# A pre-norm graph network layer on one core: the last result of a batch is joined and stored behind the next batch's first convolution, and GpSimd's transfers are planned as issued at once

## The chip, the cores and the metric

The kernel runs on one core of one Trainium2 chip. All arithmetic is in fp32. The metric is the time of one execution on the device in microseconds; lower is better. The times given are medians over several executions, and a profile is that of one further execution, taken by the hardware profiler.

In the rows of the profile, PE is TensorE (PEld is its loading of weights), DVE is VectorE, ACT is ScalarE, POOL is GpSimd and SP is SyncE. A row of a timeline gives start, length, engine, line, operation, output and inputs with their shapes, how many instructions the row stands for, and in brackets the idle time before it with what ended it.

## The reference, cut to what matters

There are 64 graphs of 256 nodes with 256 features, and a 256 x 256 adjacency matrix for each.

```python
h = jnp.maximum(_layernorm(x, axis=-1), 0.0)
x = x + gnn(h, adj, ...)

def gnn(x, mask, ...):                       # x is h here
    xc = jnp.transpose(x, (0, 2, 1))
    h = jax.nn.relu(_bn(_conv1d(xc, conv1_w, 0), ...))       # 1 tap
    h = _bn(_conv1d(h, conv2_w, 8), ...)                     # 17 taps
    x_conv = jnp.transpose(jax.nn.relu(h + xc), (0, 2, 1))
    s = x @ w_se.T + b_se                                    # 3 numbers per node
    sq = jnp.sum(s * s, axis=-1)
    dist = sq[:, :, None] + sq[:, None, :] - 2.0 * jnp.einsum('bnd,bmd->bnm', s, s)
    A = jnp.exp(-dist) * mask
    msg = jax.nn.relu(x @ w_msg.T + b_msg)
    x_nmp = jnp.einsum('bnm,bmd->bnd', A, msg)
    x_in = jnp.concatenate([x_conv, x_nmp], axis=-1)
    gi = x_in @ w_ih.T + b_ih                                # 768 = r, z, n
    gh = x @ w_hh.T + b_hh
    r = jax.nn.sigmoid(gi_r + gh_r)
    z = jax.nn.sigmoid(gi_z + gh_z)
    nn_ = jnp.tanh(gi_n + r * gh_n)
    return (1.0 - z) * nn_ + z * x
```

## The kernel before, in words

**Tiling.** A pair is two graphs (`G = 2`, 32 pairs), a batch is eight graphs or four pairs (`PB = 4`, `NB = 8` batches, numbered 0 to 7). In this text, pairs 0 to 3 are the pairs of a batch.

**The convolution of a batch.** The 17-tap convolution is done for a whole batch by a transform of length 16. VectorE splits and transforms the input (`split`, `forward`), TensorE multiplies 16 bins, each in up to three kinds of product (`begin` and `complete`, lines 908 to 937), and VectorE transforms back (`branch_back`, `odd_back`, `q_back`, `p_back`, then `join`). The transformed inputs are named `U`, `V`, `Sv` and `PT` in the trace, the transformed results `Yu` and `Yv`, and `T` is scratch. The filters of the 16 bins are worked out once, in a prologue, and lie in DRAM as `filt`. In each batch SP loads them, 256 KB at a time, into nine slots `wb` (`load_kinds`, line 872); 47 such loads make one batch. A slot is loaded again when the product that reads it is done. In the second half of the batch the same nine slots are scratch of the gates (`roles`, line 1037). At the batch's end `give` (line 1043) releases them, and `load_kinds` fills all nine for the next batch. So the first products of a batch, `acc<-Sv,wb`, can't start until the gates of the batch before have let the slots go and SP has loaded them.

**The graph work of a pair** runs beside it: `message` (features and the three numbers `s`), `embed` (transposes of them, `zT`), `affinity` (the exponential `e`, times `adj`), `aggregate` (`xnm`). From the second batch on, `hT`, the transposed normalised input of a pair, is made with DMAs: ScalarE writes `hh` (`turn_h`), a DMA transposes it into `halves`, four DMAs sort it back into `hh` (`sort_h`), and two ScalarE copies join 16-bit halves to `hT` (`join_h`). The adjacency matrix of a pair goes a similar way: a DMA transpose to `halves`, a store to DRAM (`halves_d`), four loads to `adjh`, two ScalarE copies to `adj` (`turn_adj`, `load_adj`, `join_adj`).

**The gates of a pair** (`gates`, line 1144) are twice `seven` (line 1118), which computes a 2 x 2 block product with seven instead of eight products. It holds one PSUM tile `acc`, copies it negated into a second one (ScalarE's `acc<-acc`), evicts an `aux` tile into the slot `e`, and goes on adding. ScalarE then does the nonlinear parts, and writes the result of the pair in 16-bit halves into `back`.

**The last step of a pair** (`finish`, line 1174). SP issues a DMA transpose `gn<-back`. Two ScalarE copies `back<-gn` of 1024 16-bit values for each partition join the halves. GpSimd issues, for each of the two graphs, a DMA that adds `x` from DRAM into `back` (`back<-in_x_dram`, 256 KB) and one that stores it (`out<-back`, 256 KB). The last of the 32 pairs is finished with TensorE transposes instead.

`back` and `gn` are single tiles, so the next pair's gates wait for these copies and stores.

**What sets the order.** The program isn't issued as written. A recorder (line 250) takes every operation as a task with its reads and writes, plans all of them with a list scheduler, and emits them in that order; it is why all instructions carry the one line L370 in the profile. It plans twice: the prologue, and all batches together. Each task has a modelled cost and a due time `late`, which is worked out backwards from the modelled start of each TensorE instruction. Among tasks that could start first on an engine it takes the one due first. A DMA is placed on one modelled channel (`self.dma`), and on one of two sets of eight lanes, one for GpSimd and one for all others. A DMA that isn't due within `CALM = 20` us of the point that TensorE has reached is held back until the modelled channel is free, less 1 us (lines 419 and 420):

```python
                if self.pace + self.CALM < t.late < math.inf:
                    now = max(now, self.dma - 1.0)
```

The planned order is fixed for each engine. On the chip, an engine runs its instructions in that order, and waits on semaphores for what it reads or overwrites.

**The order around the change.** In the loop over batches (lines 1248 to 1382), `finish` of the batch's first three pairs stands behind their gates (lines 1328, 1346, 1365). That of pair 3 stands at the start of the next batch, ahead of all products (line 1252). Products end with `complete(7)` (line 1298), behind which `p_back` and `q_factors` follow.

Of the kernel before, what the change touches and what calls it, by code (L numbers as in the profile page):

```python
# [14 lines left out]
U16 = mybir.dt.uint16  # L15
AF = mybir.ActivationFunctionType
ALU = mybir.AluOpType
# [10 lines left out]
class Slots:  # L28
# [3 lines left out]
    def __init__(self, t, A, n, E):  # L32
        self.t = t.rearrange("p (a c n e) -> p a c n e", a=A, c=2, n=n)
# [216 lines left out]
class Recorder:  # L250
# [15 lines left out]
    def __init__(self, nc):  # L266
        self.nc, self.tasks, self.live, self.masks = nc, [], {}, {}
        self.first, self.planned, self.dma = None, 0, 2.3
        self.lanes = [deque([0.0] * self.LANES) for _ in range(2)]
        self.free = dict.fromkeys(self.LAG, 0.0)  # L270
        for name in ("tensor", "vector", "scalar", "gpsimd", "sync"):
            setattr(self, name, Proxy(self, name))

# [59 lines left out]
    def record(self, engine, op, args, kw):  # L333
        method = getattr(getattr(self.nc, engine), op)
        out = kw["out"] if "out" in kw else args[0]
        ins = [v for v in list(args) + list(kw.values()) if isinstance(v, bass.AP) and v is not out]
        n = 1
        for s in out.shape[1:]:
            n *= s
        size = 0  # L340
        if op.startswith("dma"):
            if "transpose" in op:
                size, cost = 2.5, self.TURN
            elif "accum_op" in kw:
                size, cost = 2.3, 1.0
            else:
                k = max(self.share(out, ins[0]), 10 if engine == "gpsimd" else 1)
                run = min(self.run(v) for v in (out, ins[0]))
                size = n * out.shape[0] * WIDTH[out.dtype] * 16 / k / 330e3 * max(1, 1400 / run)
                cost = 0.35 if k > 10 and run > 1024 else 0.62  # L350
        elif engine == "tensor":
            cost = n / 597 + 0.006
            if op == "transpose":
                cost = out.shape[-1] / 1170
            elif args[1].shape[0] < 32:
                cost = 0.23
        elif engine == "vector":
            cost = {"bn_stats": 0.33, "bn_aggr": 0.07}.get(op, n / 960 + 0.07)
            if op == "tensor_mul" and n == 256:
                cost = 0.5  # L360
        elif engine == "scalar":
            cost = n / 1400 + (0.2 if op == "activation" else 0.12)
            if out.dtype == U16:
                cost = n / 860
            elif len(out.shape) == 3 and op == "activation" and n == 256:
                cost = 0.49
        else:
            cost = 1.1 if self.planned == 0 else 7.0 if ALU.pow in args else 2.0
        k = len(self.tasks)
        self.tasks.append(Task(engine, lambda: method(*args, **kw), cost, size, self.first))  # L370
        if self.first is not None:
            self.first += 1
        for v in ins:
            self.access(k, v, False)
        self.access(k, out, True)
        return k
# [7 lines left out]
    def plan(self, fixed=False):  # L384

        T, new = self.tasks, range(self.planned, len(self.tasks))
        self.planned = len(T)
        total = 0.0
        for k in new:
            t = T[k]  # L390
            for p in t.preds:
                T[p].succs.append(k)
            if t.engine == "tensor":
                t.late = total
                total += t.cost
        for k in reversed(new):
            t = T[k]
            for s in t.succs:
                t.late = min(t.late, T[s].late - self.lag(t, T[s]) - self.cost(t))
            if t.first is not None:  # L400
                t.late = t.first - 1e6
        ready, free = {e: [] for e in self.LAG}, self.free
        left = {}

        def enable(k):
            at = max((T[p].done + self.lag(T[p], T[k]) for p in T[k].preds), default=0.0)
            ready[T[k].engine].append((at, k))
        for k in new:
            left[k] = sum(p in left for p in T[k].preds)
            if not left[k]:  # L410
                enable(k)
        order = []
        self.pace = 0.0

        def when(e, at, t):
            now = max(free[e], at)
            if t.size:
                now = max(now, self.lanes[e == "gpsimd"][0])
                if self.pace + self.CALM < t.late < math.inf:
                    now = max(now, self.dma - 1.0)  # L420
            return now

        def commit(k, e, at, now):
            t = T[k]
            ready[e].remove((at, k))
            t.begin = now
            free[e] = t.done = now + t.cost
            if e == "tensor":
                self.pace = max(self.pace, t.late)
            if t.size:  # L430
                if t.cost == self.TURN:
                    free[e] = max(free[e], self.dma + 1.1)
                self.dma = max(self.dma, now + 1.6) + t.size
                t.done = self.dma + 1.1
                lanes = self.lanes[e == "gpsimd"]
                lanes.popleft()
                lanes.append(t.done)
            order.append(k)
            for s in t.succs:
                left[s] -= 1  # L440
                if not left[s]:
                    enable(s)
        while fixed and len(order) < len(new):
            k = new[len(order)]
            e = T[k].engine
            at = next(at for at, j in ready[e] if j == k)
            commit(k, e, at, max(free[e], at, self.lanes[e == "gpsimd"][0] if T[k].size else 0.0))
        while len(order) < len(new):
            best = []
            for e in ready:  # L450
                cand = [(when(e, at, T[k]), T[k].late, k, at) for at, k in ready[e]]
                if cand:
                    now = min(cand)[0]
                    best.append((now, min(c[1:] for c in cand if c[0] <= now + 1e-9), e))
            now, (_, k, at), e = min(best)
            commit(k, e, at, now)
        return order
# [25 lines left out]
def kernel(  # L483
# [18 lines left out]
    nc = Recorder(tc.nc)  # L502
    P = 128
    B, N, D = x.shape
    G = 2
    GB = 8
    PB = GB // G
    NB = B // GB
    NP = B // G
    DC = D // P  # L510
# [71 lines left out]
    def rows(t, g):  # L582
        return t[g].rearrange("(b h c) d -> h b (c d)", h=L // 2, c=MC)

    def row_tile(t, g):
        return t[:, g * MC:(g + 1) * MC, :].rearrange("p c d -> p (c d)")
# [5 lines left out]
    def chunk(t, g, c):  # L592
        return t[:, g * N + c * P:g * N + (c + 1) * P]
# [121 lines left out]
    p = aux()  # L715
# [457 lines left out]

    def finish(i):
        if i + 1 < NP:
            y = back.rearrange("p (q d) -> p q d", d=D)
            t = gn_tile.rearrange("p c n -> p (c n)").bitcast(U16)
            nc.sync.dma_start_transpose(out=t.rearrange("p (k n) -> p k n", n=P), in_=back.bitcast(U16))
            v = y.bitcast(U16).rearrange("p q (c d j) -> p j c q d", c=DC, j=2)
            u = t.rearrange("p (c j q d) -> p j c q d", j=2, c=DC, d=P)  # L1180
            for j in range(2):
                nc.scalar.copy(v[:, j], u[:, j])
            for g in range(G):
                nc.gpsimd.dma_start(out=row_tile(y, g), in_=rows(x, G * i + g), accum_op=ALU.add)
                nc.gpsimd.dma_start(out=rows(out, G * i + g), in_=row_tile(y, g))
            return
        for g in range(G):
            p = aux()
            for c in range(MC):
                for dc in range(DC):  # L1190
                    transpose(p[:, c * D + dc * P:c * D + (dc + 1) * P], chunk(tr_tile[:, dc], g, c))
            nc.vector.tensor_add(row_tile(x_rows, g), p, row_tile(x_rows, g))
            nc.sync.dma_start(out=rows(out, G * i + g), in_=row_tile(x_rows, g))

    FIRST = PARTS[1][1]
    steps = deque((m, g) for g in range(FIRST) for m in range(len(PASSES)))
# [48 lines left out]
    gn_tile, tr_tile = (late.tile([P, DC, W], FP, name=n) for n in ("gn", "tr"))  # L1245
    back = late.tile([P, DC * W], FP, name="back")
    hh, halves = (late.tile([P, 2 * MC, W], U16, name=n) for n in ("hh", "halves"))
    for b in range(NB):
        i = b * PB
        nxt = i + PB  # L1250
        if b > 0:
            finish(i - 1)
# [43 lines left out]
        if b > 0:  # L1296
            load_adj(i + 2)
        complete(7)
        fft.p_back(Yu, T)
        fft.q_factors(Yu)  # L1300
        roles()
# [128 lines left out]
```

## Time and profile before

| what | before |
| --- | --- |
| median of 3 executions | 1739.63 us (1739.28 to 1740.79) |
| profiled execution | 1734.89 us |
| its span, first to last instruction | 1733.1 us |
| mean granted TensorE clock | 0.986 |
| TensorE matmuls busy | 1678.7 us (97%) |
| VectorE busy | 1461.7 us (84%) |
| ScalarE busy | 1038.5 us (60%) |
| GpSimd busy | 254.6 us (15%) |
| DMA moved | 260.90 MB, mean 151 GB/s |
| `back<-gn` copies on ScalarE | 62, 1348 ns each |
| `back<-in_x_dram` on GpSimd's queue | 62, 256 KB each, median 7.5 us from issue to landing |
| `out<-back` on GpSimd's queue | 62, 256 KB each, median 4.5 us |
| `wb<-filt` on SP's queue | 376, 256 KB each |

Busy times are those of the profiled execution. The engines run beside each other, so their shares of the span don't add up to 100%. TensorE is the one that is nearly always busy; its remaining idle time, 54 us in all, is spread over the eight batches. The time of the profiled execution is the one to compare with its span; the median is of other executions of the same program.

### The profile page before, as it was taken

The page shows a single profiled execution, that of the slowest core. Times are in us where ns is not written, and L with a number is a line of the kernel's source. Part 1 is how long each engine was busy: PE and PEld are TensorE (multiplying, and loading weights), DVE is VectorE, ACT ScalarE, POOL GpSimd, SP SyncE. Part 2 cuts the span into 40 slices and gives each one's busy share as a digit, 9 for nine tenths or more (in the row PEclk, how much of TensorE's full clock was granted, in tenths as well). Part 3 has the DMA queues.
Part 4 walks back from the last instruction along what each step waited for, and adds up shares of the span by engine and source line. Part 5 has one row for each costly group of instructions (what it writes and reads, how often), then busy time and mean ns, then how long its engine had stood idle before and what let it go on. Part 6 is the DMA issues. An engine that isn't in the chain of part 4 may idle for free.

```text
span 1733.1 us, 26180 instructions
## 1 busy us (share of the span) xinstructions
PE 1678.7 (97%) x8998; PEld 1427.0 (82%) x8998; DVE 1461.7 (84%) x3400; ACT 1038.5 (60%) x1949; POOL 254.6 (15%) x246
## 2 busy tenths in 40 slices
PE   8999999999999999999999999999999999999996
PEld 6788878888789788888888887897888978898885
DVE  7959999699897898798986988968988889879443
ACT  3536666487656766576654766567566665547543
POOL 3211320002110221102110031102211022100010
PEclk9999999999999999999999999999999999999998
DMA  9982475865668465684558655684656847374122
GB/s 222 284 277 75 102 141 118 278 147 117 131 161 258 103 138 122 205 202 92 127 110 255 166 99 119 146 269 101 141 114 188 231 90 136 69 250 113 22 52 49
DMA packets 326457, 260.90 MB, mean 151 GB/s; under 512 B 204808, under 2 KB 252196, under 8 KB 326323
## 3 DMA queue, kind: packets, MB, share of 16 engines
q1 hardware_dynamic: 293818, 213.72, 46.6%
q0 software_dynamic: 29568, 42.84, 13.0%
q10 hardware_dynamic: 2937, 2.66, 0.7%
q8 instruction: 71, 1.16, 0.3%
q14 instruction: 63, 0.52, 0.1%
HBM read 156.03 MB, written 43.78 MB: 115 GB/s over the span
## 4 chain that ended last, share of the span: by engine, by line
PE 87%; DMA 5%; DVE 5%; ACT 2%; issue 1%; SPq 0%; POOL 0%; ACTq 0%; DVEq 0%; POOLq 0%
PE acc L370 60%; PE aux L370 27%; DMA wb<-filt 2%; DVE V L370 1%; DMA filt<-fo 1%; DVE T L370 1%; DMA hh<-halves 1%; DMA T<-in_x_dram 0%; ACT e L370 0%; DVE acc L370 0%; DVE tr L370 0%; DVE e L370 0%; DVE gn L370 0%; DMA x<-in_x_dram 0%; ACT back L370 0%
## 5 line engine op out<-in xcount | busy, mean ns | idle before, releaser
L370 PE MATMUL acc<-wb,w_ih 128*128 128x256 f32 x768 | 192.4, 379 | 0.0
L370 POOL DMA_DIRECT2D back<-in_x_dram x62 | 62.8, 1147 | 772.0 <-ACT back L370 772.0
L370 PEld LDWEIGHTS acc<-wb,w_ih 128*128 128x128 f32 x768 | 145.9, 190 | 19.8
L370 POOL TENSOR_TENSOR rstd<-rstd,neg_half 128x4 f32<-128x4 f32 x32 | 96.0, 2999 | 390.6 <-DVE shift L370 225.4
L370 PE MATMUL aux<-wb,w_x 128*128 128x256 f32 x576 | 141.3, 384 | 4.0 <-ACT e L370 3.2
L370 PE MATMUL acc<-wb,w_x 128*128 128x256 f32 x576 | 137.0, 382 | 7.5 <-DVE acc L370 7.5
L370 DVE SCALAR_TENSOR_TENSOR V<-T,V 128x128 f32<-128x128 f32 (+2 forms) x448 | 140.5, 375 | 0.0
L370 PEld LDWEIGHTS acc<-wb,w_x 128*128 128x128 f32 x576 | 107.9, 190 | 34.5 <-DVE acc L370 14.2
L370 PEld LDWEIGHTS aux<-wb,w_x 128*128 128x128 f32 x576 | 108.1, 191 | 23.6 <-ACT e L370 6.0
L370 PE MATMUL acc<-V,wb 128*128 128x128 f32 x1024 | 119.9, 277 | 5.0 <-DMA wb<-filt 3.8
L370 PE MATMUL aux<-w_msg,hT 128*128 128x259 f32 x512 | 121.5, 382 | 1.2 <-ACT fo L370 1.2
L370 DVE TENSOR_TENSOR T<-Yv 128x512 f32<-128x512 f32 (+1 forms) x80 | 42.5, 580 | 94.9 <-ACT Yv L370 94.3
L370 PEld LDWEIGHTS acc<-V,wb 128*128 128x128 f32 x1024 | 117.6, 194 | 5.9 <-DMA wb<-filt 4.4
L370 PEld LDWEIGHTS acc<-U,wb 128*128 128x128 f32 x1024 | 116.9, 192 | 0.9
L370 PE MATMUL acc<-U,wb 128*128 128x128 f32 x1024 | 117.1, 275 | 0.0
L370 PE MATMUL aux<-hT,w_c 128*128 128x512 f32 x224 | 106.9, 596 | 3.9 <-ACT e L370 2.7
L370 PE MATMUL acc<-wb,w_hh 128*128 128x256 f32 x384 | 110.0, 381 | 0.1
L370 PE MATMUL acc<-Yv,w_ih 128*128 128x256 f32 x384 | 109.6, 381 | 0.1
L370 PEld LDWEIGHTS aux<-w_msg,hT 128*128 128x128 f32 x512 | 96.3, 190 | 16.1 <-ACT fo L370 1.6
L370 PE MATMUL acc<-hT,w_hh 128*128 128x256 f32 x384 | 106.5, 384 | 3.2 <-ACT acc L370 3.2
L370 PE MATMUL acc<-xnm,w_ih 128*128 128x256 f32 x384 | 104.8, 382 | 0.0
L370 ACT COPY back<-gn 128x1024 uint16<-128x1024 uint16 x62 | 81.0, 1348 | 37.8 <-DMA gn<-back 37.8
(179 smaller groups left out, 3849.9 us busy)
## 6 DMA issues: line engine op xcount, KB each, us to landing
wb<-filt SPq DMA_DIRECT2D x376, 256.0 KB
back<-in_x_dram POOLq DMA_DIRECT2D x62, 256.0 KB, 7.5
out_dram<-back POOLq DMA_DIRECT2D x62, 256.0 KB, 4.5
x<-in_x_dram SPq DMA_DIRECT2D x58, 256.0 KB
halves_d<-halves SPq DMA_DIRECT2D x28, 512.0 KB
adjh<-halves_d SPq DMA_DIRECT2D x112, 128.0 KB
hh<-halves SPq DMA_DIRECT2D x108, 128.0 KB
filt<-fo POOLq DMA_DIRECT2D x18, 252.0 KB, 6.6
```

Source lines behind the costliest of these rows:

```text
L370: self.tasks.append(Task(engine, lambda: method(*args, **kw), cost, size, self.first))
```

## The change

Two things change. First, the rule that holds a DMA back until the modelled channel is free no longer applies to DMAs that GpSimd issues. Second, `finish` of a batch's pair 3 issues only its DMA transpose where it stood. Its two copies, two adds and two stores are a function `deliver`, which for pair 3 is recorded behind `complete(7)` of the next batch. While it is recorded, each of its tasks gets one more predecessor in the plan, `behind`, the ScalarE task recorded last before it (the last copy of `complete(7)`). That predecessor counts for the planner's order alone and makes no semaphore. For the other pairs, `finish` calls `deliver` at once, with the same operations in the same order as before.

```diff
@@ Recorder.__init__
         self.free = dict.fromkeys(self.LAG, 0.0)
+        self.last, self.behind = {}, None
@@ Recorder.record
         self.tasks.append(Task(engine, lambda: method(*args, **kw), cost, size, self.first))
+        self.last[engine] = k
+        if self.behind is not None:
+            self.tasks[k].preds.add(self.behind)
@@ Recorder.plan
             if t.size:
                 now = max(now, self.lanes[e == "gpsimd"][0])
-                if self.pace + self.CALM < t.late < math.inf:
+                if e != "gpsimd" and self.pace + self.CALM < t.late < math.inf:
                     now = max(now, self.dma - 1.0)
@@ finish
         if i + 1 < NP:
-            y = back.rearrange("p (q d) -> p q d", d=D)
             t = gn_tile.rearrange("p c n -> p (c n)").bitcast(U16)
             nc.sync.dma_start_transpose(out=t.rearrange("p (k n) -> p k n", n=P), in_=back.bitcast(U16))
-            v = y.bitcast(U16).rearrange("p q (c d j) -> p j c q d", c=DC, j=2)
-            u = t.rearrange("p (c j q d) -> p j c q d", j=2, c=DC, d=P)
-            for j in range(2):
-                nc.scalar.copy(v[:, j], u[:, j])
-            for g in range(G):
-                nc.gpsimd.dma_start(out=row_tile(y, g), in_=rows(x, G * i + g), accum_op=ALU.add)
-                nc.gpsimd.dma_start(out=rows(out, G * i + g), in_=row_tile(y, g))
+            if i % PB < PB - 1:
+                deliver(i)
             return
+
+    def deliver(i):
+        y = back.rearrange("p (q d) -> p q d", d=D)
+        t = gn_tile.rearrange("p c n -> p (c n)").bitcast(U16)
+        v = y.bitcast(U16).rearrange("p q (c d j) -> p j c q d", c=DC, j=2)
+        u = t.rearrange("p (c j q d) -> p j c q d", j=2, c=DC, d=P)
+        for j in range(2):
+            nc.scalar.copy(v[:, j], u[:, j])
+        for g in range(G):
+            nc.gpsimd.dma_start(out=row_tile(y, g), in_=rows(x, G * i + g), accum_op=ALU.add)
+            nc.gpsimd.dma_start(out=rows(out, G * i + g), in_=row_tile(y, g))
@@ the loop over batches
         complete(7)
+        if b > 0:
+            nc.behind = nc.last["scalar"]
+            deliver(i - 1)
+            nc.behind = None
         fft.p_back(Yu, T)
```

## The prediction

> **What bounds the kernel now.** I read the page's first part, then TensorE's timeline for its idle stretches, then the clock in short windows around them, then who was late there. First part of the page (busy us, share of the span, instructions):
>
> ```profile
> PE 1678.7 (97%) x8998; PEld 1427.0 (82%) x8998; DVE 1461.7 (84%) x3400; ACT 1038.5 (60%) x1949; POOL 254.6 (15%) x246
> ```
>
> TensorE's own instructions, 1679 us, can't be touched by this change: both programs hold the same 4574 of them. So only two things can move: the 54 us in which TensorE stands, and time in which it runs slowly. The timeline of TensorE shows that the largest waits recur where one batch ends and the next begins (start, length, operation; in brackets the idle time before it):
>
> ```profile
> 510.17 0.71 PE L370 MATMUL aux<-zT 9*128 9x256 f32 x8
> 511.29 3.81 PE L370 MATMUL acc<-Sv,wb 128*128 128x128 f32 x32 [0.40 <-ACT e L370]
> ...
> 914.85 0.71 PE L370 MATMUL aux<-zT 9*128 9x256 f32 x8
> 918.62 6.67 PE L370 MATMUL acc<-Sv,wb 128*128 128x128 f32 x32 [3.05 <-DMA wb<-filt]
> ```
>
> The same 32 matmuls take 3.81 us after a wait of 0.40 and 6.67 us after one of 3.05. The windows view (length, PE busy, clock, DMA share, GB/s) says why: the granted clock is halved after the long wait.
>
> ```profile
> 511.00:513.00 2.00, 1.72 (x15) 1.00 0.87 281
> ...
> 918.00:920.00 2.00, 1.38 (x6) 0.50 0.80 308
> 920.00:922.00 2.00, 2.00 (x12) 0.50 0.26 49
> ```
>
> To price wait and slow clock together I take, at each boundary, the time from the last `zT` group to the first `acc<-U,wb` group, which holds the same work: 31.45 us (batch 0 to 1: 305.22 to 336.67), 27.03 (510.17 to 537.20), 29.57, 31.60, 29.22, 29.27, and 26.31 for the last. What separates the cheap boundaries from the dear ones stands on ScalarE and GpSimd. The two joining copies of pair 2 of the batch:
>
> ```profile
> 491.44 2.56 ACT L370 COPY back<-gn 128x1024 uint16<-128x1024 uint16 x2 [3.16 <-DMA gn<-back]
> ...
> 895.31 1.35 ACT L370 COPY back<-gn 128x1024 uint16<-128x1024 uint16 x1 [1.93 <-DMA gn<-back]
> 900.99 1.34 ACT L370 COPY back<-gn 128x1024 uint16<-128x1024 uint16 x1
> ```
>
> and the transfers that follow them on GpSimd's queue:
>
> ```profile
> 494.30 1.96 POOL L370 DMA_DIRECT2D back<-in_x_dram  x2 [22.50 <-ACT back L370]
> 500.75 0.64 POOL L370 DMA_DIRECT2D out_dram<-back  x1 [4.49 <-DMA back<-in_x_dram]
> 502.76 0.63 POOL L370 DMA_DIRECT2D out_dram<-back  x1 [1.37 <-DMA back<-in_x_dram]
> ...
> 903.07 1.96 POOL L370 DMA_DIRECT2D back<-in_x_dram  x2 [27.30 <-ACT back L370]
> 909.53 0.64 POOL L370 DMA_DIRECT2D out_dram<-back  x1 [4.50 <-DMA back<-in_x_dram]
> 911.54 0.63 POOL L370 DMA_DIRECT2D out_dram<-back  x1 [1.37 <-DMA back<-in_x_dram]
> ```
>
> SP issues the first `wb<-filt` of the new batch at 506.81 and 911.50. Where the copies are adjacent the last store leaves 4.05 us ahead of these loads; where two gate activations stand between them it leaves 0.04 us behind. The other boundaries agree: apart at 713, 1122 and 1325 (dear), adjacent at 1528 (cheap). At 306 a third form: GpSimd's power waited 16.02 us for VectorE ahead of the second add (306.95), and the last store left at 317.34, amid the loads.
>
> **What the Trainium skill says.** "DMA: Bandwidth & Descriptors", section "Issuing engines are not separate DMA queues": transfers of all issuing engines share the same 16 DMA engines and interleave. The trace agrees: GpSimd's queue takes 20.6% of DMA time in 905 to 935 and 10.5% in 500 to 530. "TensorE: Matmul & The Clock Gate", section "HAM oscillation": a DMA wait that leaves the array idle makes the next work start at half clock. The page puts this at gaps over 3.4 us; here 1.96 us (at 1122.69) already brought 0.50, and the measurement decides. Its section on the array's architecture calls ScalarE and VectorE strict FIFO, so a copy behind a waiting instruction waits too; the 895.31/900.99 pair shows that.
>
> **The change part by part.** The order of the built programs, engine by engine, tells where things went.
>
> *The moved delivery (2 copies of 1.34 us, 2 adds, 2 stores).* In batches 2 to 6 it moves nowhere: the copies are ScalarE's instructions 651/653, 891/893 and so on in both programs. The trace shows it already late: adds at 1184.40, 62 us into the batch. In batch 1 they come 24 places earlier, in batch 7 later, into a stretch where ScalarE is idle for 3.26 us (before 1587.92) against 2.68 us of copies. TensorE has no gap there that they cause. Worth 0.
>
> *The copies of pair 2.* The new planning rule puts them next to each other at the four dear boundaries (788/791 become 788/789, and so on). ScalarE is idle for 3.10 us after the first copy (1101.9 to 1105.0), so the second fits. Adds and stores leave about 4.3 us earlier, as at 511. Bringing four boundaries to 27.03: 2.54 + 4.57 + 2.19 + 2.24 = 11.5 us; to the best one, 26.31, 14.4. I take 11.5.
>
> *Boundary 0 to 1.* Both adds and both stores now precede GpSimd's power: the adds go at about 289, the stores near 297, ahead of the loads at 301.87. 31.45 - 27.03 = 4.4 us (5.1 at best). What is late next is what the cheap boundaries show: 0.40 us on ScalarE's `e`.
>
> *Batch 0, TensorE.* Eleven matmul instructions (three `adjh,msg`, eight `w_msg,hT`; some 4.75 us at 0.43) now stand ahead of the products that waited 1.40 us at 108.12 and 0.88 at 110.16 for filters. They need nothing that is late. Gain 2.3 us.
>
> *Batch 0, the others.* VectorE gets four `w_x`/`w_ih` steps (3.8 us at 0.95) ahead of `T<-Yv`, in front of which it stood idle for 11.58 us. They wait for `w_ih`, which landed 10.4 us after 96.75, at 107.1; VectorE comes to them then. Bound 0 to 2 us, taken 0. At 226.51 TensorE waited 2.43 us for a ScalarE copy behind an `hT` copy that itself waited 3.60 us for `hh`; that chain now starts earlier. Bound 0 to 2.4, taken 1.2. Two `x` loads now stand among the filter loads of batch 0: 0 to 1.6 us (256 KB each at 319 GB/s), taken 0 since the eleven matmuls go first.
>
> *Batches 1 to 6, small swaps.* In gates of pair 0 the `hT` copy (1.35 us) now precedes `acc<-acc`, on which TensorE waits. In before, `acc` ran at 1225.15 and was first used at 1228.90. If `hh` lands by 1226.7, `acc` is done at 1228.6: no wait; if 1 us later, 0.7 us. The adj transpose now issues right behind `hh`, so I charge 0.5 us x 6 = 3 us (bounds 0 and 6). The first copies of pair 1 are now split, by two activations of 0.67: stores 1.3 us later, landing near 1290, while `back` is written next at 1297.99; 0. The `gn` and adj transposes swap on SP: the 512 KB `halves_d` store moves later by some 4 us from 1302.68, still ahead of 1320.73; 0 to 1 each, inside the range. Adj copies go ahead of two evictions while ScalarE is idle for 5.14 us; 0.
>
> **Sum.** 11.5 + 4.4 + 2.3 + 1.2 - 3 = 16.4 us. The profiled execution took 1734.89 us (span 1733.1, 1.8 around it); less 16.4 is 1718.5. The median shown is 1739.63, 4.7 above that execution; I carry the difference over: 1723. About 0.2% (3.5 us) is what a measurement here tells from no change.
>
> **Rivals.**
> 1. The stores don't cause the boundary wait; the loads are just late after the slots come free. For it: TensorE's wait is named `wb<-filt` throughout, and the slots' release sets when SP can issue. Against: seven boundaries sort by the stores. Then only batch 0 gains: 2.3 + 1.2 - 3, about 1739.
> 2. The boundaries improve by half, since the later `halves_d` store and transposes join the adds: (11.5 + 4.4)/2 + 3.5 - 3 = 8.5, about 1731.
> 3. Slower: the `hT` copy ahead of `acc` stalls. Place: gates of pair 0 in six batches. For it: batch 0 had this very order in before and paid 2.43 us at 226.51. Against: there `hh` landed some 4.2 us after its last issue, and the steady batches allow 3.9 to 4.7. With `hh` 4 us later than that, each wait costs 4 us and a halved clock 1 to 2 more: 6 x 5.5 = 33, less 19.4 gained, 13.6 slower, about 1753. It decides from 3.8 us per batch, where 23 us eat the gain and pass 0.2%.
>
> **How the numbers follow.** Forecast 0.66, rival 1 0.15, rival 2 0.11, rival 3 0.08. The forecast's own range is 1714 (14.4 + 5.1 + 4.7 and one small gap, no new wait) to 1729. With rival 2 and part of rival 1 the range is 1713 to 1737. Faster: 0.66 + 0.11 + a third of rival 1, 0.82; same: half of rival 1 and a little of 3, 0.09; slower 0.09.
>
> **What would show it.** In the changed profile: clock 1.00 at every boundary, zT to U near 27 us at all seven, pair 2's copies as x2 and its last store 4 us ahead of the first filter load; no wait at 108 and 110. I am wrong if the stores are early and the wait remains (rival 1), or if TensorE waits for ScalarE's `acc` in gates of pair 0 (rival 3).

## The result: faster by 1.3%, and the profile after

The changed kernel took 1714.32 us (median of 4 executions, 1712.77 to 1717.68) against 1739.45 us (4 executions, 1731.27 to 1740.79): a ratio of 0.9868, 95% interval 0.9834 to 0.9901. That is 23 us off 1739, between 17 and 29. The profiled execution took 1717.68 us with a span of 1715.9, so profile against profile it is 17.2 us. Instructions of the changed kernel carry the line L371. First part of its page (busy us, share of the span, instructions):

```profile
PE 1670.4 (97%) x8998; PEld 1418.1 (83%) x8998; DVE 1462.3 (85%) x3400; ACT 1040.0 (61%) x1949; POOL 229.8 (13%) x246
```

TensorE has the same number of matmuls, is busy 8.3 us less for them (the mean granted clock rose from 0.986 to 0.991), and stands 45.5 us instead of 54.4. The idle time before isn't spread evenly over the batches: 5.8 us of it lie in the prologue and 16.7 behind the last boundary (from 1553 us on). The 31.9 us in between became 22.0. The boundary of batches 3 and 4, TensorE's timeline of the changed kernel:

```profile
906.91 0.71 PE L371 MATMUL aux<-zT 9*128 9x256 f32 x8
908.36 3.97 PE L371 MATMUL acc<-Sv,wb 128*128 128x128 f32 x32 [0.73 <-ACT e L371]
```

Its windows there (length, busy time and count of PE, PEld, DVE, ACT and POOL, then clock, DMA share, GB/s):

```profile
908.00:910.00 2.00, 1.64 (x15) 1.67 (x16) 2.00 (x4) 1.77 (x6) 0.52 (x2) 1.00 0.93 330
910.00:912.00 2.00, 2.00 (x19) 1.91 (x18) 2.00 (x5) 0.98 (x2) 0.00 (x0) 1.00 0.89 265
```

The wait of 3.05 us has become 0.73, and the clock stays at 1.00 where it was 0.50. ScalarE's and GpSimd's timelines show what came first:

```profile
887.81 2.55 ACT L371 COPY back<-gn 128x1024 uint16<-128x1024 uint16 x2 [2.36 <-DMA gn<-back]
```

```profile
891.10 1.96 POOL L371 DMA_DIRECT2D back<-in_x_dram  x2 [22.79 <-ACT back L371]
899.63 0.64 POOL L371 DMA_DIRECT2D out_dram<-back  x1 [6.58 <-DMA back<-in_x_dram]
900.53 0.63 POOL L371 DMA_DIRECT2D out_dram<-back  x1 [0.26 <-DMA back<-in_x_dram]
```

The two copies are one row of x2, and the last store leaves 6.4 us ahead of the `zT` products; before, it left 3.3 us ahead of them (911.54 against 914.85). The DMA view of the 7 us from the first filter load on, in the kernel before (911.5 to 918.5):

```profile
q1 hardware_dynamic: 735, 1.35, 55.5%
q0 software_dynamic: 207, 0.46, 27.1%
...
wb<-filt SPq DMA_DIRECT2D x7, 256.0 KB
out_dram<-back POOLq DMA_DIRECT2D x1, 256.0 KB, 6.7
```

and in the changed kernel (903.5 to 910.5):

```profile
q1 hardware_dynamic: 957, 1.75, 73.7%
q0 software_dynamic: 117, 0.19, 8.5%
...
wb<-filt SPq DMA_DIRECT2D x9, 256.0 KB
```

Columns are packets, MB and share of the DMA engines; q0 is GpSimd's queue, q1 is SP's. In the 7 us at the same position SP's queue moved 1.75 MB instead of 1.35, while GpSimd's share of the DMA engines fell to a third.

The loads were not issued earlier. In all twelve profiles, at all seven boundaries, SP's first filter load leaves 3.35 or 3.36 us ahead of the `zT` products. So the moment at which the slots come free, which the prediction's rival 1 brought in, is not what separates cheap from dear.

The stretch from the last `zT` group to the first `acc<-U,wb` group, in us, for all twelve kernels (the experiments are explained below; bold where pair 2's copies stand apart, or where GpSimd's power stands between the adds):

| kernel | 0-1 | 1-2 | 2-3 | 3-4 | 4-5 | 5-6 | 6-7 |
| --- | --- | --- | --- | --- | --- | --- | --- |
| before | **31.45** | 27.03 | **29.57** | **31.60** | **29.22** | **29.27** | 26.31 |
| changed | 27.33 | 27.20 | 26.68 | 27.79 | 26.79 | 26.73 | 26.45 |
| rule alone | 26.33 | 26.60 | 26.54 | 27.34 | 26.37 | 26.43 | 26.08 |
| moved delivery alone | **29.22** | 26.30 | **28.14** | **30.08** | **28.34** | **30.12** | 26.17 |
| copies joined | **29.36** | 26.08 | 26.28 | 26.67 | 26.24 | 26.33 | 26.08 |
| copies put apart | 27.07 | 26.66 | **29.97** | **30.68** | **29.87** | **29.62** | 26.14 |
| transfers dropped | **29.90** | 26.20 | **26.36** | **26.47** | **26.40** | **27.39** | 26.09 |
| stores held | 30.64 | 28.97 | 29.47 | 29.40 | 28.94 | 29.37 | 28.83 |
| power behind the stores | 26.08 | 26.48 | **28.13** | **28.55** | **29.51** | **29.50** | 26.08 |
| rule, early part | 27.11 | 26.11 | **29.76** | **31.12** | **27.60** | **29.81** | 26.77 |
| rule, late part | **29.88** | **30.01** | 26.39 | 27.50 | 26.55 | 26.34 | 26.09 |
| rule for no queue | 29.62 | 27.95 | 26.55 | 27.33 | 26.99 | 26.86 | 26.53 |

Two rows break the pattern: in one the transfers are gone though the copies stand apart, in the other the stores are late though the copies are adjacent. Two single entries break it too: 27.60 with copies apart, where TensorE waited 1.81 us but then needed only 3.81 us for the 32 products, and 29.62 in the last row, where both copies come 4 us later than elsewhere. The last store sorts better than the copies do. Where it left at least 2.2 us ahead of SP's first filter load, the stretch is 26.1 to 28.0 us; where it left at most 0.8 us ahead, or behind, the stretch is 27.6 to 31.6.

### The profile page after: what moved, and what is told of

It reads as the page before. It is cut to its first block, busy times and chain, and to the rows that moved or that the text cites. A ratio compares the mean times of both kernels' runs of the same rounds, so it can differ in the third digit from the quotient of the medians.

```text
span 1715.9 us, 26176 instructions
## 1 busy us (share of the span) xinstructions
PE 1670.4 (97%) x8998; PEld 1418.1 (83%) x8998; DVE 1462.3 (85%) x3400; ACT 1040.0 (61%) x1949; POOL 229.8 (13%) x246
## 4 chain that ended last, share of the span: by engine, by line
PE 81%; DVE 11%; DMA 4%; ACT 3%; issue 1%; POOL 0%; SPq 0%; ACTq 0%; DVEq 0%; POOLq 0%
PE acc L371 56%; PE aux L371 25%; DVE V L371 2%; DVE T L371 2%; DVE tr L371 1%; DVE U L371 1%; DMA wb<-filt 1%; DMA filt<-fo 1%; DMA hh<-halves 1%; ACT gn L371 1%; DVE acc L371 1%; ACT zT L371 1%; DVE e L371 1%; DVE Yv L371 1%; DVE gn L371 1%
## 5 line engine op out<-in xcount | busy, mean ns | idle before, releaser
L371 PE MATMUL acc<-wb,w_ih 128*128 128x256 f32 x768 | 192.4, 379 | 0.0
L371 PEld LDWEIGHTS acc<-wb,w_ih 128*128 128x128 f32 x768 | 145.9, 190 | 19.8
L371 POOL DMA_DIRECT2D back<-in_x_dram x62 | 61.8, 1154 | 717.1 <-ACT back L371 713.8
L371 PE MATMUL acc<-wb,w_x 128*128 128x256 f32 x576 | 137.5, 383 | 11.5 <-DVE acc L371 11.5
L371 PE MATMUL aux<-wb,w_x 128*128 128x256 f32 x576 | 141.9, 384 | 2.3 <-ACT e L371 2.3
L371 DVE SCALAR_TENSOR_TENSOR V<-T,V 128x128 f32<-128x128 f32 (+2 forms) x448 | 140.6, 375 | 0.0
L371 PEld LDWEIGHTS acc<-wb,w_x 128*128 128x128 f32 x576 | 107.3, 190 | 38.1 <-DVE acc L371 19.8
L371 POOL TENSOR_TENSOR rstd<-rstd,neg_half 128x4 f32<-128x4 f32 x32 | 76.9, 2404 | 442.7 <-DVE shift L371 251.3
L371 PEld LDWEIGHTS aux<-wb,w_x 128*128 128x128 f32 x576 | 107.8, 191 | 22.4 <-ACT e L371 4.3
L371 PE MATMUL aux<-w_msg,hT 128*128 128x259 f32 x512 | 121.1, 381 | 2.7 <-ACT fo L371 2.7
L371 PE MATMUL acc<-V,wb 128*128 128x128 f32 x1024 | 117.7, 275 | 0.9 <-DMA wb<-filt 0.9
L371 PEld LDWEIGHTS acc<-U,wb 128*128 128x128 f32 x1024 | 117.1, 192 | 0.9
L371 PE MATMUL acc<-U,wb 128*128 128x128 f32 x1024 | 117.2, 275 | 0.0
L371 PEld LDWEIGHTS acc<-V,wb 128*128 128x128 f32 x1024 | 116.0, 192 | 1.3 <-DMA wb<-filt 1.3
L371 ACT COPY back<-gn 128x1024 uint16<-128x1024 uint16 x62 | 81.0, 1348 | 54.1 <-DMA gn<-back 54.1
L371 PE MATMUL acc<-Yv,w_ih 128*128 128x256 f32 x384 | 110.1, 382 | 0.9 <-ACT Yv L371 0.8
L371 PEld LDWEIGHTS aux<-w_msg,hT 128*128 128x128 f32 x512 | 96.3, 189 | 17.5 <-ACT fo L371 3.1
L371 PE MATMUL acc<-wb,w_hh 128*128 128x256 f32 x384 | 109.9, 381 | 0.0
L371 PE MATMUL aux<-hT,w_c 128*128 128x512 f32 x224 | 105.4, 594 | 2.1 <-DVE msg L371 1.6
L371 PE MATMUL acc<-hT,w_hh 128*128 128x256 f32 x384 | 105.9, 383 | 0.7 <-ACT acc L371 0.7
L371 PE MATMUL aux<-e,msg 128*128 128x256 f32 x448 | 104.4, 379 | 0.0
L371 PE MATMUL acc<-xnm,w_ih 128*128 128x256 f32 x384 | 104.4, 380 | 0.0
```

## The experiments

Each was timed beside the kernel before on its chip (medians there 1734.79, 1735.86 and 1736.36 us, of 27 to 58 executions).

**Which half of the change does it?** The rule alone:

```diff
-                if self.pace + self.CALM < t.late < math.inf:
+                if e != "gpsimd" and self.pace + self.CALM < t.late < math.inf:
```

> The kernel before with the planning rule of the change alone (GpSimd's transfers no longer held back); the last delivery stays where it was. Theory A (the gain comes from pair 2's copies becoming adjacent and from GpSimd's order at the first boundary, both of which the rule brings): all of the gain, a ratio of 0.986 to 0.990, and the seven zT-to-U stretches at 26.4 to 27.8 us as in the changed kernel. Rival B (the moved delivery brings it): within 3 us of before, four stretches at 29 to 32 us.

Measured: 1715.07 us, ratio 0.9897 (0.9869 to 0.9924), all seven stretches at 26.1 to 27.3.

The moved delivery alone (the change without that line):

> The kernel before with the moved delivery alone; the planning rule stays. It moves instructions in the last batch only. Theory A: 0 to 2 us faster (the last batch took 172.05 us from its first U product to the end after, 173.24 before), the stretches as in before. Rival B: the whole gain, some 17 to 23 us.

Measured: 1735.19 us, ratio 0.9995 (0.9982 to 1.0008); five stretches as in before. The rule does all of it that can be told from nothing. So of the two parts of the change, the moved delivery is worth nothing that these runs can tell.

**Are the copies of pair 2 the cause at the four dear boundaries?** A pass over the planned order, ahead of emission (`joins` holds the two copies of a pair):

```diff
+    def edit(self, order):
+        for i in (10, 14, 18, 22):
+            if i in self.joins and self.joins[i][1] in order:
+                j, k = sorted(self.joins[i], key=order.index)
+                order.remove(k)
+                order.insert(order.index(j) + 1, k)
+        return order
```

> The kernel before with one edit to ScalarE's order: at the four dear boundaries (batches 2 to 5) pair 2's second joining copy stands directly behind the first. Everything else is as in before. Theory A: the stretches at these four boundaries fall from 29.2 to 31.6 us to about 26.7 to 27.8, the clock there is 1.00, 12 us in all, a ratio of about 0.993. Rival C (the gain there comes from the other changes of order in the steady batches, or the loads are late anyway): within 3 us of before.

Measured: 1726.22 us, ratio 0.9954 (0.9937 to 0.9971), 8.0 us off 1734.8. The four stretches fell to 26.2 to 26.7. TensorE's timeline at the boundary of batches 3 and 4:

```profile
915.29 0.71 PE L371 MATMUL aux<-zT 9*128 9x256 f32 x8
916.41 3.81 PE L371 MATMUL acc<-Sv,wb 128*128 128x128 f32 x32 [0.40 <-ACT e L371]
```

One instruction of 1.34 us, moved past two others on an engine that is 60% busy, takes a wait and a slow clock away from TensorE.

The opposite edit in the changed kernel moves the second copy, and GpSimd's adds and stores with it, behind the next two ScalarE tasks:

```diff
+                k = max(self.joins[i], key=order.index)
+                a = order.index(k)
+                acts = [n for n in range(a + 1, len(order)) if self.tasks[order[n]].engine == "scalar"]
+                b = acts[1]
+                late = [k]
+                for t in order[a + 1:b + 1]:
+                    if self.tasks[t].preds & set(late):
+                        late.append(t)
+                order[a:b + 1] = [t for t in order[a:b + 1] if t not in late] + late
```

> The changed kernel with the opposite edit: at the same four boundaries the second joining copy is put back behind the two gate activations, with GpSimd's adds and stores following it. Theory A: 12 us of the gain are given back, a ratio to before of about 0.994 where the changed kernel has 0.987, four stretches at 29 to 32 us. Rival C: within 3 us of the changed kernel.

Measured: 1724.81 us, ratio 0.9942 (0.9921 to 0.9962): 0.0045 of the rule's 0.0103 is given back, some 8 us (0.0074, some 13 us, against the changed kernel's own ratio of 0.9868, which was measured at another time). ScalarE's timeline, GpSimd's, and then TensorE's, at the same boundary:

```profile
886.32 1.35 ACT L372 COPY back<-gn 128x1024 uint16<-128x1024 uint16 x1 [2.20 <-DMA gn<-back]
890.57 0.69 ACT L372 ACTIVATE tr<-acc,b_rz 128x512 f32<-128x512 f32 x1 [2.89 <-PE acc L372]
891.15 0.68 ACT L372 ACTIVATE wb<-acc,b_rz 128x512 f32<-128x512 f32 x1
891.72 1.35 ACT L372 COPY back<-gn 128x1024 uint16<-128x1024 uint16 x1
```

```profile
893.81 1.96 POOL L372 DMA_DIRECT2D back<-in_x_dram  x2 [26.70 <-ACT back L372]
900.27 0.64 POOL L372 DMA_DIRECT2D out_dram<-back  x1 [4.50 <-DMA back<-in_x_dram]
902.03 0.63 POOL L372 DMA_DIRECT2D out_dram<-back  x1 [1.11 <-DMA back<-in_x_dram]
```

```profile
905.59 0.71 PE L372 MATMUL aux<-zT 9*128 9x256 f32 x8
909.06 5.44 PE L372 MATMUL acc<-Sv,wb 128*128 128x128 f32 x32 [2.76 <-DVE tr L372]
```

The copy waits 4 us for its turn, as ScalarE waits 2.89 us for TensorE in front of it; the stores leave at the end of that chain; TensorE waits 2.76 us and then needs 5.44 us for what takes 3.81. The wait is put down to VectorE's `tr`, in other kernels to `gn` or to ScalarE's `e`. It is a wait for several semaphores at once, so these rows alone don't show that the filters end it; the next run bears on that.

**The traffic, or the order on ScalarE?** In the kernel before, the four transfers of those pairs are taken out of the planned order, and nothing else is moved:

```diff
+    def edit(self, order):
+        gone = {k for i in (10, 14, 18, 22) for k in self.moves.get(i, ())}
+        return [k for k in order if k not in gone]
```

> The kernel before, in which the two adds and two stores of pair 2 of batches 2 to 5 are left out (eight graphs of x are not added and not stored); all other orders, the apart copies among them, are as in before. Theory A (traffic of adds and stores amid the filter loads makes the dear boundaries): the four stretches fall to 26 to 27.5 us although the copies stay apart, 8 to 12 us in all, a ratio of 0.993 to 0.995 as for the adjacent copies. Rival D (ScalarE's order itself delays what the slots wait for, the traffic does no harm): the four stretches stay at 28 to 31 us, the ratio at 0.998 or above.

Measured: 1725.58 us, ratio 0.9950 (0.9933 to 0.9967). ScalarE's timeline still shows the copies apart:

```profile
894.07 1.35 ACT L371 COPY back<-gn 128x1024 uint16<-128x1024 uint16 x1 [1.93 <-DMA gn<-back]
898.58 0.69 ACT L371 ACTIVATE tr<-acc,b_rz 128x512 f32<-128x512 f32 x1 [3.16 <-PE acc L371]
...
899.74 1.35 ACT L371 COPY back<-gn 128x1024 uint16<-128x1024 uint16 x1
```

and TensorE's shows no wait:

```profile
913.60 0.71 PE L371 MATMUL aux<-zT 9*128 9x256 f32 x8
914.72 3.81 PE L371 MATMUL acc<-Sv,wb 128*128 128x128 f32 x32 [0.41 <-ACT e L371]
```

Leaving 1 MB of traffic out at each of the four boundaries gives as much as moving the copy (8.7 and 8.0 us). Without the transfers, the later writers of `back` have less to wait for as well. That doesn't explain it: in the kernel before, `back` is next written at 927.07, 8 us after TensorE's wait had ended at 918.62. So the copy's place matters only through the transfers that wait for it, and rival D falls.

**The stores by themselves.** The changed kernel, with work on GpSimd between adds and stores of pair 2 of each batch:

```diff
+    def hold(self, i):
+        if i % 4 == 2:
+            self.nc.gpsimd.memset(self.idle, 1.0)
+            for _ in range(HOLD):
+                self.nc.gpsimd.tensor_tensor(self.idle, self.idle, self.idle, ALU.pow)
```

> The changed kernel, in which GpSimd does ten short powers on an idle tile between the adds and the stores of pair 2 of each batch, so that the stores leave some 4 us later, with the first filter loads of the next batch; ScalarE, TensorE, VectorE and SP keep their orders, and the adds leave when they did. Theory A: the stretches grow by 1 to 4 us at all or most of the seven boundaries, 8 to 20 us in all. Rival D: within 3 us of the changed kernel (1714). Between them, under 8 us, it would be the adds and not the stores that collide.

Measured: 1738.04 us, ratio 1.0018 (1.0004 to 1.0032), which gives back the whole gain. All seven stretches grew, by 1.6 to 3.3 us, 16.7 in all; profile against profile it is 17.6 us. By the ratios (1.0018 against 0.9868, from different times) it would be some 26 us; what that has beyond the stretches wasn't traced. GpSimd's timeline:

```profile
901.54 1.96 POOL L373 DMA_DIRECT2D back<-in_x_dram  x2 [22.32 <-ACT back L373]
...
903.70 17.39 POOL L469 TENSOR_TENSOR bn_rows<-bn_rows 20x4 f32<-20x4 f32 x10
921.05 1.31 POOL L373 DMA_DIRECT2D out_dram<-back  x2
```

The ten powers took 17.4 us where I had counted on 10.3 from the 1.03 us of a single `rstd` power, so the stores left 7 us later than meant, in the middle of the loads and not at their head. The wait moved accordingly, from the first products to those 12 us later (TensorE's timeline):

```profile
918.66 3.81 PE L373 MATMUL acc<-Sv,wb 128*128 128x128 f32 x32 [0.41 <-ACT e L373]
...
927.35 1.16 PE L373 MATMUL acc<-V,wb 128*128 128x128 f32 x8 [0.42 <-DMA wb<-filt]
930.60 2.05 PE L373 MATMUL acc<-V,wb 128*128 128x128 f32 x16 [2.08 <-DMA wb<-filt]
```

Stores alone, with the adds where they were, are enough for the wait. The powers themselves do not slow VectorE there: its instructions from 899.84 to 922.52 are those of the changed kernel from 889.22 to 911.89, each of the same length and at the same distance of 10.6 us. In the kernel with the copies put apart only the stores can have met the loads as well: a store waits for its add to land, the last one left at 902.03, and SP issued the first filter load at 902.23 (914.18 in the kernel with held stores, 7 us ahead of them).

**The first boundary.** In the kernel before, the second add and both stores of pair 2 of batch 0 go ahead of GpSimd's power on `rstd`:

```diff
+            first, *rest = sorted(self.moves[2], key=order.index)
+            order = [k for k in order if k not in rest]
+            n = order.index(first) + 1
+            order[n:n] = rest
```

> The kernel before with one edit to GpSimd's order: at the boundary of batches 0 and 1 the second add and both stores stand ahead of the power on rstd, as in the changed kernel. Theory A: that stretch falls from 29.2 to 31.5 us to about 27, 2 to 4.4 us, a ratio of 0.9975 to 0.999; the rest as before. Rival B2 (that wait is for filters that are late anyway): no change.

Measured: 1733.09 us, ratio 0.9982 (0.9965 to 0.9999), 3.1 us with an interval of 0.2 to 6.1; the stretch is 26.08.

**Batch 0 and the rest.** `mark` is the number of the first task of batch 1; the rule is lifted for GpSimd's transfers below it in one kernel, and from it on in the other:

```diff
-                if self.pace + self.CALM < t.late < math.inf:
+                if not (e == "gpsimd" and k < self.mark) and self.pace + self.CALM < t.late < math.inf:
```

> The kernel before with the rule lifted for GpSimd's transfers of the prologue and batch 0 alone. Orders up to the first boundary are those of the changed kernel, and pair 2's copies stay apart at the four later boundaries. Theory A: what is left of the gain when the four boundaries are taken off: 2.8 us for the first boundary, as measured for GpSimd's order alone, and 5.0 for batch 0, which the three traces with the changed order took from the first product to the last zT in 206.6 us on the mean, against 211.5 in three with the old order; in all about 8 us, a ratio of 0.994 to 0.997. Rival E (batch 0's order is worth nothing and its traces differ by chance): 3 us, 0.998.

Measured: 1725.54 us, ratio 0.9937 (0.9915 to 0.9959), 10.9 us, between 7 and 15. The ratio is just under the range that was expected; theory A's 8 us lies inside the interval, and rival E's 3 us does not.

> The kernel before with the rule lifted for GpSimd's transfers of batches 1 to 7 alone. Batch 0 keeps its old order; the copies of pair 2 are adjacent at the four dear boundaries, but come apart at boundary 1 to 2, where they were adjacent before. Theory A: minus 8 us for the four, plus 2 to 3 for boundary 1 to 2, which turns dear (28.5 us or more): 5 to 7 us faster, 0.996 to 0.998. Were the steady swaps of order worth something by themselves (rival F), it would differ from that by over 3 us.

Measured: 1730.88 us, ratio 0.9965 (0.9952 to 0.9978), 6.1 us as theory A has it. Boundary 1 to 2, cheap in all other kernels but the one with held stores, was dear here at 30.01, with its copies apart: TensorE's timeline shows the slow 5.44 again.

```profile
518.17 5.44 PE L371 MATMUL acc<-Sv,wb 128*128 128x128 f32 x32 [2.48 <-DMA wb<-filt]
```

The two parts together, 17.0 us, are the rule's 17.9 within the intervals, though the late part pays some 3 us at boundary 1 to 2 (30.01 against 26.60) that the whole rule doesn't.

**The rule for no queue at all** (`CALM` from 20 to 1e9, in the kernel before):

> The kernel before with the holding-back rule lifted for all engines' transfers, SP's too. If transfers are best planned at once on any queue, it is as fast as the changed kernel or faster, 1705 to 1716 us. If the rule does its work for SP's queue (keeping transposes and x loads from going ahead of what TensorE waits for), it is slower than the changed kernel, and new waits for DMAs show in TensorE's timeline. I hold the second the likelier, 1720 to 1745 us.

Measured: 1728.29 us, ratio 0.9964 (0.9950 to 0.9978). Six boundaries are at 26.5 to 28.0, but new waits stand inside the batches (TensorE's timeline):

```profile
763.84 1.85 PE L370 MATMUL acc<-PT,wb 128*128 128x128 f32 x8 [2.26 <-DMA wb<-filt]
```

The 16 us around it hold two transposes, a 512 KB store, three loads of `adjh` and two of `x`, all on SP's queue, with only six filter loads among them. In the kernel before no product of `PT` waits for a filter. The six batches between the seven boundaries took 1061.3 us, against 1043.6 in the kernel before, which eats what the boundaries gain. Lifting the rule for GpSimd alone is the better of the two.

## Why the prediction was right, point by point

The forecast was 16.4 us off the profiled execution; profiles gave 17.2, the medians 23 (17 to 29), so by the medians 16.4 lies just below the interval. The time foretold was 1723 us in a range of 1713 to 1737; the 1714.32 us measured lie close to its lower end. By its steps:

- **The copies of pair 2: 11.5 us.** Right in cause. In the traces the four stretches add up to 118.1 us with copies apart (mean of five kernels) and 106.7 with copies adjacent (mean of four), 11.4 us. Timed by itself the edit gave 8.0 (5 to 11), so the price from the traces lies just above that. Why the two differ isn't settled. The stores also left less early than I had said: 2.3 to 3.8 us ahead of the first filter load at these boundaries, not 4. At the boundary of batches 3 and 4 the adds took 8.4 us to land instead of 6.9, with the 512 KB `halves_d` store beside them. So rival 2 had something right, but of small size: the four stretches add up to 108.0 us in the changed kernel and 105.5 with the copies joined alone, where that store comes earlier.
- **Boundary 0 to 1: 4.4 us.** 3.1 us when timed alone. The stretches with the old order average 29.96 (five kernels), those with the new one 26.78 (five, held stores aside): 3.2 us. The profile that I priced it from had the dearest of the five.
- **Batch 0: 2.3 + 1.2 = 3.5 us.** Too small. From the first product to the next `zT`, six kernels with the old order took 212.5 us on the mean and five with the new one 206.3: 6.2 us. One term that was mis-sized is the wait at 226.51, which I took at half of its bound. In the kernel before, ScalarE and then TensorE:

```profile
224.63 1.33 ACT L370 COPY hT<-hh 128x1024 uint16<-128x1024 uint16 x1 [3.60 <-DMA hh<-halves]
225.83 0.62 ACT L370 ACTIVATE acc<-acc 128x512 f32<-128x512 f32 x1
```

```profile
226.51 0.70 PE L370 MATMUL acc<-hT,w_hh 128*128 128x256 f32 x2 [2.43 <-ACT acc L370]
```

The wait is 1.6 to 2.5 us in the six kernels with the old order, and it is gone whole in the five with the new one. The changed kernel, ScalarE first, then TensorE where it needs `acc`:

```profile
212.43 1.36 ACT L371 COPY hT<-hh 128x1024 uint16<-128x1024 uint16 x1 [1.22 <-DMA hh<-halves]
...
223.32 0.58 ACT L371 ACTIVATE acc<-acc 128x512 f32<-128x512 f32 x1
```

```profile
224.13 0.59 PE L371 MATMUL acc<-hT,w_hh 128*128 128x256 f32 x2
```

`hT` no longer stands right ahead of `acc` but 11 us earlier, so its wait for `hh` harms nobody; no idle time stands before the matmul. The filter waits at 108 and 110 are gone too, but for 0.36 us in one kernel; with the old order they were 1.2 to 3.2 us, and in two of the six the products behind them took 5.44 us in place of 3.81. The last 1 us or so was not traced to a row, and no run takes the swaps of batch 0 one by one.

- **The swap of `hT` and `acc` in six batches: a loss of 3 us.** No wait of TensorE came of it. Of the changed kernel, ScalarE and then TensorE:

```profile
1209.62 1.34 ACT L371 COPY hT<-hh 128x1024 uint16<-128x1024 uint16 x1 [0.35 <-DVE tr L371]
1211.02 0.58 ACT L371 ACTIVATE acc<-acc 128x512 f32<-128x512 f32 x1
```

```profile
1213.35 1.03 PE L371 MATMUL acc<-hT,w_hh 128*128 128x256 f32 x4
```

ScalarE doesn't wait for `hh` there, and `acc` is done at 1211.60, 1.75 us before the product that must wait for it. In three of the six batches ScalarE does wait for `hh`, by 0.57, 1.02 and 1.46 us, and `acc` is still done 0.8 us or more ahead.

The margin was thinner than the prediction had it. It counted from the end of `acc` to `acc<-wb,w_hh` at 1228.90. But the row at 226.51 shows that `acc<-hT,w_hh` waits already, as it goes on adding to the tile that ScalarE's copy reads. In the kernel before, ScalarE and then TensorE:

```profile
1225.15 0.58 ACT L370 ACTIVATE acc<-acc 128x512 f32<-128x512 f32 x1
```

```profile
1227.17 1.03 PE L370 MATMUL acc<-hT,w_hh 128*128 128x256 f32 x4
```

That is a slack of 1.4 us in place of 3.2, so that the swap cost so little was in part luck. Rival 3 needed `hh` late by nearly 4 us to be slower in all. Outside the stretches, batches 1 to 6 took 1043.9 us on the mean in six kernels with the old order there and 1045.7 in five with the new one; these 1.9 us are not traced to a row.

- **The moved delivery: 0.** 0.9 us with an interval of minus 1.4 to 3.1.
- **The carry-over to the median.** I added 4.7 us, as the profiled execution was that much below the median of three. The changed kernel's profiled execution lies 3.4 us above its own median, and the kernel before had medians of 1735 to 1736 in later runs. The first product starts anywhere from 92.7 to 101.1 us in the twelve profiles: the prologue alone swings by more than most of the steps above. One profile's offset from a median is no constant to carry over.

Summed over all traces the parts come to 11.4 + 3.2 + 6.2 - 1.9 = 18.9 us, 2.5 more than the 16.4 of the forecast: 2.7 from batch 0 and 1.1 from the swaps, less 1.3 at the boundaries. The one pair of profiles shows 17.2 us as follows: the seven stretches gave 15.5, batch 0 gave 5.4 and the last batch 1.2, batches 1 to 6 took 1.3 more, and the prologue 3.5 more, as the changed kernel's first product started at 97.47 us there and that of before at 94.02. The sum had left the prologue out. So the close fit of 16.4 to 17.2 is partly chance; that the boundaries and batch 0 give the gain is not.

## What to carry to other kernels

If a wait for a load recurs once in a loop, and is cheap in some turns and dear in others, sort the turns by what else is on the DMA engines in those microseconds; the cause can be a small instruction on another engine that lets someone's stores go 4 us later. In a planner, holding a transfer back because it isn't due can put it where the burst comes that everything waits for: in this kernel stores of finished results went best at once; with the rule lifted for loads and transposes as well, new waits came up inside the batches.

## What the runs showed of the hardware that wasn't expected

The halved clock after a wait isn't a matter of the wait's length alone. The same 32 products took 6.67 us after 3.05 and 5.44 after 2.48 and 2.76, but 3.81 after 2.63 us in the kernel with the moved delivery alone. The same boundary of batches 4 and 5, first in the kernel before, then in that kernel:

```profile
1122.69 5.39 PE L370 MATMUL acc<-Sv,wb 128*128 128x128 f32 x32 [1.96 <-ACT e L370]
...
1122.18 3.81 PE L371 MATMUL acc<-Sv,wb 128*128 128x128 f32 x32 [2.63 <-DVE tr L371]
```

The windows view of TensorE in the same two (length, busy, clock, DMA share, GB/s):

```profile
1124.00:1126.00 2.00, 2.00 (x11) 0.50 0.46 153
...
1122.00:1124.00 2.00, 1.82 (x16) 1.00 0.71 273
```

The Trainium skill, "TensorE: Matmul & The Clock Gate", section on HAM oscillation, has this at gaps over 3.4 us; here the clock was halved after 1.96 us (before, at 1122.69) and full after 2.63, so no length between decides it alone. What does decide it stays open.

GpSimd's power has no one price. In the kernel with held stores, ten of them took 17.1 to 18.2 us at the seven boundaries. Late in the last batch the same ten took 10.7:

```profile
1706.46 10.71 POOL L469 TENSOR_TENSOR bn_rows<-bn_rows 20x4 f32<-20x4 f32 x10
```

VectorE was busy for all of the 17.3 us from 903.7 on, and for 1.4 of the 10.8 us from 1706.4 on. That the two go together in this run is all that is shown. The single power on `rstd` took 1.03 us in many places and up to 9.30 in others in the kernel before (mean of 32: 3.0), so the 1.03 that I had counted with was its best case.
